# Loading a 3327 x 3327 int32 graph as bytes: casts on GpSimd replaced by casting transfers

## The chip, the cores and the metric

One core of one Trainium2 chip runs the kernel. The metric is device time in microseconds (us) of one execution; the kernel before was run three times.

## What is computed

Two layers on x (3327 rows of 256 floats), each a graph attention and a feed-forward part with residuals. The part that concerns us is the first graph attention, with two heads of 128 columns:

```python
e = leaky_relu(s1[:, None, :] + s2[None, :, :], 0.2)
e = where(adj[:, :, None] == 1, e, NEG)
att = softmax(e, axis=1)
h_prime = einsum('ijh,jhc->ihc', att, W3h)
```

`adj` is a 3327 x 3327 int32 matrix of zeros and ones (44.3 MB). After it come a mixture of 16 experts (two for each row), a second graph attention on the same graph with one head of 256 columns, and 30 steps of a recurrent feed-forward block.

## The kernel before

Rows are handled in 26 tiles of 128 (NT = 26, NP = 3328), and in pairs: tile 2c has the even rows and tile 2c+1 the odd rows of a stretch of 256. The last tile has 127 rows.

**Graph.** The whole graph stays in SBUF, transposed, as one byte for each edge (`adjT`, the tile `adj_pairs`), and both attentions read it there. `transpose_graph` (L227 to L251) fills it, one row tile i after the other, in two halves of 1664 and 1663 columns:

- L239: SP issues a load of int32 values into `raw` (three buffers, 832 KB each),
- L247, L249: GpSimd fills the padding of `bytes` (the last tile's last rows; the last column) with zeros,
- L250: GpSimd casts `raw` to 8-bit floats in `bytes` (two buffers),
- L251: when both halves are there, SP issues a DMA transpose of `bytes`, read as pairs of bytes, into the columns of `adj_pairs` that belong to row tile i.

**Projection.** Before the loop over edges, `project` normalizes x (L115, L116 on VectorE, the inverse deviation `rstd` at L106 on GpSimd, the scaling `xn` at L119 on VectorE), transposes it on TensorE (L149) and multiplies it by the weights (L157). VectorE puts the result into `wh` (L306) and the scores (L310, L311). `wv` and `shift` (L291 to L303) are made from weights that GpSimd's queue loads.

**Attention.** `attend` (L180 to L220) runs over row groups, in the first layer of 4, 6, 6, 6 and 4 tiles (L41), in each over heads and in each over the 26 tiles j of neighbours. One step j is: ScalarE makes `e` (L201, relu of a broadcast row of scores), VectorE adds and multiplies by the graph's bytes (L206, `pT`), TensorE multiplies each row tile of `pT` by `wh` (L211, `acc`). L206 reads for each j all columns of the group, so a group can't start before all its row tiles have been transposed: group 0 needs tiles 0 to 3, group 1 tiles 4 to 9, group 2 tiles 10 to 15, group 3 tiles 16 to 21, group 4 tiles 22 to 25. At the end of a group and head come the reciprocal (L219) and the residual (L320).

**Order.** Each engine executes its instructions in one order, which a scheduler lays down beforehand from the order of the program and planned durations; the code doesn't write it out. Casts of the graph and `rstd` of L106, for instance, stand mixed in GpSimd's order. An instruction that waits holds up all behind it on its engine. So also on the queues: SP's holds the loads of x (L70), of the graph, the transposes, and later the copies of x for the experts (L390); GpSimd's holds the loads of weights (L274, L286, L98).

Of the kernel before, what the change touches and what calls it, by code (L numbers as in the profile page):

```python
# [9 lines left out]
I32 = mybir.dt.int32  # L10
# [7 lines left out]
P = 128  # L18
# [8 lines left out]
def gat_moe_gat_recurrent_ffn(ctx: ExitStack, tc: tile.TileContext, a: dict, out: bass.AP):  # L27
    nc = tc.nc
    N, D = a["x"].shape
    KD = D // P  # L30
    NT = (N + P - 1) // P
    NP = NT * P
# [12 lines left out]
    def rows(t):  # L45
        return P if t < NT - 2 else (REST + 1 - t % 2) // 2

    def spread(n):

        cut = n - n % 16  # L50
        return [r for r in ((0, cut), (cut, n)) if r[0] < r[1]]

    def every_partition(ap, n):

        return bass.AP(tensor=ap.tensor, offset=ap.offset, ap=[[0, P], [1, n]])
# [83 lines left out]
    def project(wv, n_out, finish, ps_n, ps_p, work):  # L139

        for ts in groups:
            n = len(ts)
            xn = work.tile([P, G, D], F32, name="xn")
            normalized([x[:, t, :] for t in ts], [xn[:, j, :] for j in range(n)], EPS)
            hT = work.tile([P, KD, G * P], F32, name="hTg")
            for k in range(KD):
                pt = ps_n.tile([P, G * P], F32, name="pt")
                for j in range(n):
                    nc.tensor.transpose(pt[:, j * P : (j + 1) * P], xn[:, j, k * P : (k + 1) * P], ident)  # L149
                if k == 0:  # L150
                    nc.vector.tensor_copy(hT[:, k, : n * P], pt[:, : n * P])
                else:
                    nc.scalar.copy(hT[:, k, : n * P], pt[:, : n * P])
            for j, t in enumerate(ts):
                p = ps_p.tile([P, 512], F32, name="pp")
                for k in range(KD):
                    nc.tensor.matmul(  # L157
                        p[:, :n_out], lhsT=hT[:, k, j * P : (j + 1) * P], rhs=wv[:, k, :],
                        start=(k == 0), stop=(k == KD - 1),
                    )  # L160
                finish(t, p)
# [62 lines left out]
    adj_pairs = graph.tile([P, PAIRS, NP], BF16, name="adjT")  # L224
    adjT = adj_pairs.bitcast(FP8).rearrange("p c (i b) -> p c i b", b=2)

    def transpose_graph(ts, pools):  # L227

        raw_p, cast_p = pools
        half = NP // 2  # L230
        for i in ts:
            pr = rows(i)
            b = cast_p.tile([P, NP], FP8, name="bytes")
            for lo in (0, half):
                real = min(half, N - lo)
                raw = raw_p.tile([P, half], I32, name="raw")
                for r0, r1 in spread(pr):
                    first = i // 2 * 2 * P + i % 2 + 2 * r0
                    nc.sync.dma_start(  # L239
                        raw[r0:r1, :real],  # L240
                        bass.AP(
                            tensor=a["adj"].tensor, offset=a["adj"].offset + first * N + lo,
                            ap=[[2 * N, r1 - r0], [1, real]],
                        ),
                    )
                if pr < P:
                    nc.gpsimd.memset(b[96:P, lo : lo + half], 0.0)  # L247
                if real < half:
                    nc.gpsimd.memset(b[:, lo + real : lo + half], 0.0)  # L249
                nc.gpsimd.tensor_copy(b[:pr, lo : lo + real], raw[:pr, :real], saturate=False)  # L250
            nc.sync.dma_start(adj_pairs[:, :, i * P : (i + 1) * P], b.bitcast(BF16), transpose=True)  # L251


    with ExitStack() as st:
        H = 2
        C = D // H
        keep = st.enter_context(tc.tile_pool(name="keep0", bufs=1))
        wh = keep.tile([P, NT, H, C + 1], F32, name="wh")
        sc = Scores(keep, H)
        gpools = (  # L260
            st.enter_context(tc.tile_pool(name="raw", bufs=3)),
            st.enter_context(tc.tile_pool(name="cast", bufs=2)),
        )
        nc.vector.memset(wh[:, :, :, C : C + 1], 1.0)
        with ExitStack() as pre:
            work = pre.enter_context(tc.tile_pool(name="work0", bufs=2))
            hold = pre.enter_context(tc.tile_pool(name="hold0", bufs=1))
            ps_n = pre.enter_context(tc.tile_pool(name="ps0n", bufs=2, space=PSUM))
            ps_p = pre.enter_context(tc.tile_pool(name="ps0p", bufs=2, space=PSUM))
            ps_v = pre.enter_context(tc.tile_pool(name="ps0v", bufs=1, space=PSUM))  # L270

            def once(name, shape, src):
                t = hold.tile(shape, F32, name=name)
                nc.gpsimd.dma_start(t, src)  # L274
                return t

            w1 = once("gw1", [P, H, D], a["W1"].rearrange("(h c) d -> c h d", c=P))
            w2 = once("gw2", [P, H, D], a["W2"].rearrange("(h c) d -> c h d", c=P))
            aT = once("gaT", [P, 2, H], a["aT"].rearrange("(s c) h -> c s h", c=P))
            b1 = once("gb1", [P, H], a["b1"])  # L280
            b2 = once("gb2", [P, H], a["b2"])
            b3 = once("gb3", [P, D], every_partition(a["b3"], D))


            wv = hold.tile([P, KD, D + 2 * H], F32, name="wv")
            nc.gpsimd.dma_start(wv[:, :, :D], a["W3T"].rearrange("(k p) c -> p k c", p=P))  # L286
            for h in range(H):
                for k in range(KD):
                    for s, w in ((0, w1), (1, w2)):
                        pv = ps_v.tile([P, 1], F32, name="pv")  # L290
                        nc.tensor.matmul(  # L291
                            pv, lhsT=w[:, h, k * P : (k + 1) * P], rhs=aT[:, s, h : h + 1], start=True, stop=True
                        )
                        nc.vector.tensor_copy(wv[:, k, D + s * H + h : D + s * H + h + 1], pv)
            shift = hold.tile([P, H], F32, name="shift")
            for h in range(H):
                pv = ps_v.tile([P, 1], F32, name="pv")
                for s, b in ((0, b1), (1, b2)):
                    nc.tensor.matmul(
                        pv, lhsT=b[:, h : h + 1].to_broadcast([P, P]), rhs=aT[:, s, h : h + 1],  # L300
                        start=(s == 0), stop=(s == 1),
                    )
                nc.vector.tensor_copy(shift[:, h : h + 1], pv)  # L303

            def split0(t, p):
                nc.vector.tensor_tensor(  # L306
                    wh[:, t, :, :C], p[:, :D].rearrange("p (h c) -> p h c", h=H),
                    b3.rearrange("p (h c) -> p h c", h=H), ALU.add,
                )
                nc.vector.tensor_tensor(sc.s1[:, t, :], p[:, D : D + H], shift, ALU.add)  # L310
                nc.vector.tensor_copy(sc.s2[:, t, :], p[:, D + H : D + 2 * H])  # L311
                if t % G == G - 1 or t == NT - 1:
                    sc.finish(t - t % G, t + 1)

            project(wv, D + 2 * H, split0, ps_n, ps_p, work)
            transpose_graph(range(NT), gpools)

        def add_scaled(t, pr, h, po, r):
            xs = x[:pr, t, h * C : (h + 1) * C]
            nc.vector.scalar_tensor_tensor(xs, po, r, xs, op0=ALU.mult, op1=ALU.add)  # L320

        with ExitStack() as run:
            pools = (
                run.enter_context(tc.tile_pool(name="edge0", bufs=3)),
                run.enter_context(tc.tile_pool(name="ps0r", bufs=1, space=PSUM)),
                run.enter_context(tc.tile_pool(name="ps0o", bufs=2, space=PSUM)),
            )
            attend(sc, wh, H, groups0, 3, add_scaled, pools)
# [8 lines left out]
    with ExitStack() as st:  # L337
# [7 lines left out]
        first = hold.tile([P, SLOTS], F32, name="first")  # L345
# [3 lines left out]
        with ExitStack() as pre:  # L349
# [33 lines left out]
            for ts in groups:  # L383
# [30 lines left out]
                def gcol(name):  # L414
                    return gate.tile([P, G], F32, name=name)
# [12 lines left out]
                m1, r1, m2, r2 = gcol("m1"), gcol("r1"), gcol("m2"), gcol("r2")  # L428
# [183 lines left out]
    with ExitStack() as st:  # L612
# [31 lines left out]
        with ExitStack() as run:  # L644
            fin = run.enter_context(tc.tile_pool(name="fin2", bufs=2))

            def add_elu(t, pr, h, po, r):
# [9 lines left out]
            pools = (  # L657
                run.enter_context(tc.tile_pool(name="edge2", bufs=4)),
                run.enter_context(tc.tile_pool(name="ps2r", bufs=1, space=PSUM)),
                run.enter_context(tc.tile_pool(name="ps2o", bufs=1, space=PSUM)),  # L660
            )
# [145 lines left out]
```

## Time and profile before

| what | value |
|---|---|
| median of three runs | 2431.76 us (2431.38 to 2441.16) |
| profiled execution | 2433.84 us, its span 2432.1 us |
| TensorE busy | 2077.5 us, 85% |
| VectorE busy | 1544.4 us, 63% |
| ScalarE busy | 1068.8 us, 44% |
| GpSimd busy | 1024.5 us, 42% |
| mean granted TensorE clock | 0.942 of full speed |
| DMA traffic | 147.87 MB, HBM read 167.29 MB |

By stages: the projection ends at about 69 us, the first attention runs from there to about 426 us, the experts follow, then the second attention, and the recurrent block fills most of the last 900 us. The graph is loaded from 6.2 us (first load issued) to 227.5 us (last transpose issued). Sixteen DMA engines move the data; a load of half a row tile of the graph took a median of 6.8 us from issue to landing, a transpose 4.6 us.

How to read it: a group of instructions is given with its line, engine, operation, tiles (out<-in), shapes and count, then the busy time in us, the mean time of one in ns, and the time that its engine sat idle just before these instructions, with what ended it. The chain of work that ended last is followed back from the last instruction, at each step to what released it. "PEclk" is the share of full clock that TensorE was granted.

### The profile page before, as it was taken

The page shows a single profiled execution, that of the slowest core. Times are in us where ns is not written, and L with a number is a line of the kernel's source. Part 1 is how long each engine was busy: PE and PEld are TensorE (multiplying, and loading weights), DVE is VectorE, ACT ScalarE, POOL GpSimd, SP SyncE. Part 2 cuts the span into 40 slices and gives each one's busy share as a digit, 9 for nine tenths or more (in the row PEclk, how much of TensorE's full clock was granted, in tenths as well). Part 3 has the DMA queues.
Part 4 walks back from the last instruction along what each step waited for, and adds up shares of the span by engine and source line. Part 5 has one row for each costly group of instructions (what it writes and reads, how often), then busy time and mean ns, then how long its engine had stood idle before and what let it go on. Part 6 is the DMA issues. An engine that isn't in the chain of part 4 may idle for free.

```text
span 2432.1 us, 32383 instructions
## 1 busy us (share of the span) xinstructions
PE 2077.5 (85%) x10906; PEld 1695.3 (70%) x10906; DVE 1544.4 (63%) x4363; ACT 1068.8 (44%) x1373; POOL 1024.5 (42%) x743
## 2 busy tenths in 40 slices
PE   6889999610888888877999986999999999999998
PEld 4789999500444444545888875788888888888887
DVE  7899777610222222227555557988888888888888
ACT  1556566000222222212443344666666666666664
POOL 4544000233333333331000003777777777777774
PEclk9999999555999999998999997999999999999999
DMA  7987000101565665632000000000000000000001
GB/s 239 313 253 211 14 1 14 55 12 23 143 167 143 165 168 141 152 77 64 1 1 1 1 1 3 1 1 1 1 1 1 1 1 1 1 1 1 1 1 57
DMA packets 127889, 147.87 MB, mean 61 GB/s; under 512 B 61614, under 2 KB 97744, under 8 KB 127724
## 3 DMA queue, kind: packets, MB, share of 16 engines
q1 hardware_dynamic: 112364, 126.19, 17.0%
q0 software_dynamic: 15360, 19.62, 5.0%
q8 instruction: 87, 1.43, 0.2%
q14 instruction: 78, 0.64, 0.1%
HBM read 167.29 MB, written 19.30 MB: 77 GB/s over the span
## 4 chain that ended last, share of the span: by engine, by line
PE 62%; DVE 15%; DMA 10%; ACT 8%; issue 4%; POOL 1%; SPq 0%; ACTq 0%; DVEq 0%; POOLq 0%
PE acc L211 24%; PE po L745 19%; PE pa L589 5%; DMA lists<-number,ati 4%; DMA rows<-table_x,which 3%; ACT zT L741 3%; PE po L601 3%; DVE v L711 3%; DVE stats L737 3%; PE pt L739 3%; PE pb L589 3%; DVE pT L206 2%; DVE h L750 2%; ACT th L729 1%; PE pp L157 1%
## 5 line engine op out<-in xcount | busy, mean ns | idle before, releaser
L745 PE MATMUL po<-wc,zT 128*128 128x256 f32 x3120 | 711.0, 385 | 42.8 <-ACT zT L741 41.2
L745 PEld LDWEIGHTS po<-wc,zT 128*128 128x128 f32 x3120 | 586.8, 191 | 147.3 <-ACT zT L741 71.4
L211 PE MATMUL acc<-wh,pT 128*128 128x129 f32 (+1 forms) x4056 | 619.7, 315 | 53.1 <-DVE pT L206 49.4
L211 PEld LDWEIGHTS acc<-wh,pT 128*128 128x128 f32 x4056 | 570.7, 194 | 100.5 <-DVE pT L206 36.7
L206 DVE SCALAR_TENSOR_TENSOR pT<-e,part,adjT 128x512 f32<-128x512 f32 (+2 forms) x442 | 399.6, 921 | 165.4 <-PE acc L211 152.1
L731 POOL TENSOR_TENSOR th<-th,h 128x1024 f32<-128x1024 f32 (+1 forms) x210 | 463.7, 2209 | 82.7 <-ACT th L729 82.6
L201 ACT ACTIVATE e<-rb,minus,full 128x512 f32<-128x512 f32 (+2 forms) x442 | 358.5, 840 | 238.2 <-DVE pT L206 177.4
L750 DVE SCALAR_TENSOR_TENSOR h<-po,rr,bb 128x256 f32<-128x256 f32 x780 | 323.5, 477 | 32.5 <-PE po L745 26.5
L737 DVE BATCH_NORM_STATS2 stats<-z 128x6 f32<-128x256 f32 x780 | 286.4, 414 | 77.7 <-ACT z L732 77.7
L729 ACT ACTIVATE th<-h 128x1024 f32<-128x1024 f32 (+1 forms) x210 | 209.1, 996 | 283.8 <-DVE h L750 136.7
L720 POOL TENSOR_TENSOR rr<-v,neg_half 128x4 f32<-128x4 f32 (+1 forms) x210 | 204.5, 974 | 175.2 <-DVE v L716 173.6
L741 ACT COPY zT<-pt 128x1024 f32<-128x1024 f32 (+1 forms) x210 | 198.2, 945 | 76.7 <-PE pt L739 76.7
L732 ACT ACTIVATE z<-th 128x1024 f32<-128x1024 f32 (+1 forms) x210 | 210.4, 1002 | 9.1 <-DVE stats L737 6.7
L603 DVE TENSOR_SCALAR y<-po,col 128x256 f32<-128x256 f32 x67 | 32.4, 484 | 279.3 <-PE po L601 279.3
L739 PE MATMUL pt<-ident,z 128*128 128x128 f32 x1560 | 193.0, 275 | 16.4 <-ACT z L732 16.4
L739 PEld LDWEIGHTS pt<-ident,z 128*128 128x128 f32 x1560 | 180.1, 143 | 29.7 <-ACT z L732 17.8
L106 POOL TENSOR_TENSOR rstd<-ve,neg_half 128x4 f32<-128x4 f32 (+1 forms) x28 | 28.2, 1006 | 401.3 <-DVE ve L104 363.1
L604 POOL DMA_INDIRECT acc<-y,to x67 | 105.8, 1580 | 189.7 <-DVE y L603 97.1
L584 ACT COPY hT<-pt 128x256 f32<-128x256 f32 x67 | 24.9, 372 | 352.4 <-PE pt L583 219.9
L589 PE MATMUL pa<-ew,hT 128*128 128x512 f32 x268 | 146.9, 631 | 34.8 <-ACT hT L584 34.8
L711 DVE TENSOR_TENSOR v<-stats 128x4 f32<-128x4 f32 (+1 forms) x210 | 134.1, 638 | 7.1
L601 PEld LDWEIGHTS po<-ew,hidT 128*128 128x128 f32 x536 | 96.4, 189 | 57.6 <-ACT hidT L598 44.9
(180 smaller groups left out, 1618.9 us busy)
## 6 DMA issues: line engine op xcount, KB each, us to landing
ew<-in_w_dram SPq DMA_DIRECT2D x201, 512.0 KB
raw<-in_adj_dram SPq DMA_DIRECT2D x25, 832.0 KB, 6.8
raw<-in_adj_dram SPq DMA_DIRECT2D x25, 831.5 KB
acc<-x SPq DMA_DIRECT2D x26, 128.0 KB, 1.8
x<-acc SPq DMA_DIRECT2D x26, 128.0 KB, 3.3
table_x<-row SPq DMA_DIRECT2D x6, 520.0 KB, 3.1
x<-in_x_dram SPq DMA_DIRECT2D x6, 512.0 KB, 10.8
out_dram<-h SPq DMA_DIRECT2D x6, 512.0 KB, 2.8
```

What stands on the lines that cost most here:

```text
L201: nc.scalar.activation(e[:, : n * P], rb[:, :n, :].rearrange("p c q -> p (c q)"), AF.Relu, scale=sc.full[:, j, h : h + 1], bias=sc.minus[: ...
L206: nc.vector.scalar_tensor_tensor(pT[:, : n * P], e[:, : n * P], sc.part[:, j, h : h + 1], adjT[:, j // 2, ts[0] * P : (ts[-1] + 1) * P, j ...
L211: nc.tensor.matmul(po[c], lhsT=pT[:, c * P : (c + 1) * P], rhs=wh[:, j, h, :], start=(j == 0 and c % per_bank == 0), stop=(j == NT - 1), s ...
L589: nc.tensor.matmul(p, lhsT=hT[:, k, :], rhs=w[:, k, :], start=(k == 0), stop=(k == KD - 1))
L729: nc.scalar.activation(th[:, :n, :], hs, AF.Tanh, scale=1.0 / S)
L731: nc.gpsimd.tensor_tensor(th[:, :n, :], th[:, :n, :], hs, ALU.add)
L732: nc.scalar.activation(z[:, :n, :], th[:, :n, :], AF.Silu, scale=1.0 / S)
L737: nc.vector.bn_stats(stats[:, j, :], z[:, j, :])
L739: nc.tensor.transpose(pt[:, j, k, :], z[:, j, k * P : (k + 1) * P], ident)
L741: nc.scalar.copy(zT[:, :n, :, :], pt[:, :n, :, :])
L745: nc.tensor.matmul(po[:, j, :], lhsT=zT[:, j, k, :], rhs=wc[:, k, :], start=(k == 0), stop=(k == KD - 1),)
L750: nc.vector.scalar_tensor_tensor(h[:, ts[0] + j, :], po[:, j, :], rr[:, j : j + 1], bb, op0=ALU.mult, op1=ALU.add)
```

## The change

The loads of int32 into `raw` and GpSimd's casts are gone. GpSimd's queue issues transfers that read int32 from HBM and write 8-bit floats into `bytes`, so the transfer itself converts. Each row is cut at column 2048 into two transfers (2048 and 1279 columns), for all 128 rows of a tile at once; the last tile's 127 rows are split into 112 and 15, so it has four. The padding is filled first. `raw` and its three buffers vanish, `bytes` has four buffers instead of two. The transpose of L251 is as it was and stays on SP's queue.

```diff
-    def transpose_graph(ts, pools):
-
-        raw_p, cast_p = pools
-        half = NP // 2
+    def transpose_graph(ts, cast_p):
+
         for i in ts:
             pr = rows(i)
             b = cast_p.tile([P, NP], FP8, name="bytes")
-            for lo in (0, half):
-                real = min(half, N - lo)
-                raw = raw_p.tile([P, half], I32, name="raw")
-                for r0, r1 in spread(pr):
-                    first = i // 2 * 2 * P + i % 2 + 2 * r0
-                    nc.sync.dma_start(
-                        raw[r0:r1, :real],
+            if pr < P:
+                nc.gpsimd.memset(b[96:P, :], 0.0)
+            nc.gpsimd.memset(b[:, N:], 0.0)
+            for r0, r1 in spread(pr):
+                first = i // 2 * 2 * P + i % 2 + 2 * r0
+                for lo in range(0, N, 2048):
+                    hi = min(N, lo + 2048)
+                    nc.gpsimd.dma_start(
+                        b[r0:r1, lo:hi],
                         bass.AP(
                             tensor=a["adj"].tensor, offset=a["adj"].offset + first * N + lo,
-                            ap=[[2 * N, r1 - r0], [1, real]],
+                            ap=[[2 * N, r1 - r0], [1, hi - lo]],
                         ),
                     )
-                if pr < P:
-                    nc.gpsimd.memset(b[96:P, lo : lo + half], 0.0)
-                if real < half:
-                    nc.gpsimd.memset(b[:, lo + real : lo + half], 0.0)
-                nc.gpsimd.tensor_copy(b[:pr, lo : lo + real], raw[:pr, :real], saturate=False)
             nc.sync.dma_start(adj_pairs[:, :, i * P : (i + 1) * P], b.bitcast(BF16), transpose=True)
...
-        gpools = (
-            st.enter_context(tc.tile_pool(name="raw", bufs=3)),
-            st.enter_context(tc.tile_pool(name="cast", bufs=2)),
-        )
+        cast_p = st.enter_context(tc.tile_pool(name="cast", bufs=4))
...
-            transpose_graph(range(NT), gpools)
+            transpose_graph(range(NT), cast_p)
```

## The prediction

> **What bounds the kernel now.** I read the chain of work that ended last first, then the groups of instructions with shapes kept apart, for 70 to 232 us (the graph is being loaded) and for 232 to 440 us (the same loop, graph resident), then one tile's instructions, the chain in order of time, and the DMA packet records. The chain over the whole span says that TensorE sets the end, VectorE second:
>
> ```profile
> PE 62%; DVE 15%; DMA 10%; ACT 8%; issue 4%; POOL 1%; SPq 0%; ACTq 0%; DVEq 0%; POOLq 0%
> ```
>
> The change touches only what runs up to 232 us. In the groups of 70 to 232 us (count | busy us, mean ns | idle before) the edge products of L206 take 1352 and 1122 ns, beside GpSimd casts of 1.8 us:
>
> ```profile
> L206 DVE SCALAR_TENSOR_TENSOR pT<-e,part,adjT 128x768 f32<-128x768 f32 x64 | 83.1, 1352 | 3.5 <-PE acc L211 2.9 <-ACT e L201 0.6
> L206 DVE SCALAR_TENSOR_TENSOR pT<-e,part,adjT 128x512 f32<-128x512 f32 x52 | 56.0, 1122 | 2.4 <-ACT e L201 0.8
> L250 POOL CAST bytes<-raw 128x1664 fp8e4<-128x1664 int32 x19 | 35.3, 1860 | 30.4 <-DMA raw<-in_adj_dram 30.4
> ```
>
> The same instructions from 232 us on, with GpSimd idle:
>
> ```profile
> L206 DVE SCALAR_TENSOR_TENSOR pT<-e,part,adjT 128x768 f32<-128x768 f32 x93 | 94.0, 1017 | 27.8 <-PE acc L211 25.5 <-ACT e L201 2.2
> L206 DVE SCALAR_TENSOR_TENSOR pT<-e,part,adjT 128x512 f32<-128x512 f32 x52 | 38.6, 750 | 5.8 <-PE acc L211 0.5 <-ACT e L201 0.2
> ```
>
> Min/median/max of the 52 products in the first row group (69 to 132 us), then in the last (374 to 426 us), which has the same shape:
>
> ```profile
> L206 DVE SCALAR_TENSOR_TENSOR pT<-e,part,adjT x52: 737/751/2078, 70.0 to 130.2; 128x512 f32<-128x512 f32 x52
> ```
>
> ```profile
> L206 DVE SCALAR_TENSOR_TENSOR pT<-e,part,adjT x52: 732/752/753, 375.4 to 423.3; 128x512 f32<-128x512 f32 x52
> ```
>
> The medians agree; the first group has a tail up to 2078 ns, as long as a cast. A product that meets a cast waits it out. The tail is on the chain, and so are two stalls in the projection before it (start, us):
>
> ```profile
> 39.02 3.23 DVE xn L119 x2
> ...
> 54.24 1.46 DVE xn L119
> ...
> 75.65 2.02 DVE pT L206
> ...
> 80.88 2.06 DVE pT L206
> ```
>
> **The change, part by part.** Each sum is made against the profiled execution (2433.84 us, span 2432.1), 2.1 us over the median of 2431.76.
>
> *Casts removed (52 of L250, 91.5 us of GpSimd).* Row group 0 runs from 69.23 to 132.23 us on the chain, 63.0; group 4, same size without casts, from 374.57 to 425.65, 51.1: 11.9 us less. Late next there is PE: its 104 products of one head take 23.4 us, VectorE's 26 x 0.75 = 19.5, ScalarE's 26 x 0.78 = 20.2. Group 1 (six tiles) takes 132.23 to 214.95, 82.7; groups 2 and 3 take 79.0 and 79.7: 3.4 us less. VectorE loses 64 x 335 ns = 21 us to casts in the six-tile groups, but PE is the longer engine there (some 36 us a head against 26 x 1.02 = 26.5), so most of it is hidden. Together -15.3.
>
> In the projection the xn scalings of L119 have a median of 408 ns; on the chain the pair at 39.02 takes 3.23 instead of 0.73 us, the one at 54.24 1.46 instead of 0.40, the pair at 56.1 1.5 instead of 0.73: -4.4. PE ran dry at both places and then had a clock of 0.52 (43.4 to 46.8 us) and 0.50 (57.0 to 63.8); at that clock eight products of L157 took 3.41 us, elsewhere 1.92. That is 1.5 + 2 x 0.95 = 3.4 us that may go or stay; I take half, -1.7.
>
> *Transfers moved from SP to GpSimd's queue.* 54 issues leave SP; 54 come to GpSimd, two a tile (four for the last). GpSimd's plain issues in the trace take 0.54 to 0.89 us, so some 40 us, against 91.5 of casts. Behind them in GpSimd's order stand the rstd of L106; two are on the chain (37.96, 52.33), each perhaps behind one issue: +0.75 each, +1.5. A tile's issue now also waits for one of four "bytes" buffers, that is for a transpose four tiles back; behind that wait stand later issues and rstd. The memsets (26 of 0.10 us, 3 us for the last tile) stay. On SP only transposes and x loads stay; a transpose now waits for a transfer instead of a cast. The first transfers can start behind the weight loads, at 6.4 us, beside the x loads rather than behind them on SP; x may land later; VectorE idles 2.3 us for PE's shift at 26 to 28 us, which hides that much. I take nothing.
>
> Do issues stall VectorE as casts do? Lowest price nothing, highest the same share, 40/91.5 = 44% of the gain given back. The rows nearest: three issues from 16.82 to 18.68 us, beside which xn took 0.46 and 0.75 for two, the undisturbed times within 0.06. I take nothing. [...]
>
> *The cast inside the transfer: the unknown.* No row shows a casting DMA. Packet records: a plain 6656-byte packet took 252 ns (median) on SP's queue, 4096 bytes 159 ns on GpSimd's, so the same 26 bytes/ns from either; a 256-byte transpose packet 18 ns; a 1024-byte packet of the accumulating scatter of L604, the only DMA here that computes, 101 ns against 45 plain. Per tile and DMA engine there are 8 rows of 13.3 KB and 104 transpose packets (1.9 us). Low end, plain rate: 8 x 504 ns + 1.9 = 5.9 us a tile; in the trace two tiles take 14 us with the DMA engines full, 7. High end by the nearest row, the accumulating one: 13308/1024 x 101 = 1313 ns a row, 10.5 + 1.9 = 12.4 us a tile. At X us a tile, tile k (from 0) has landed at 6.4 + (k+1)X + 4.6 (transposes land in 4.6). With the gains above, group 0 starts at 64.6 and group 1 at 115.7; it needs tile 9, so 11 + 10X <= 115.7: X up to 10.5 costs nothing, because the matmuls of earlier groups hide the loading (groups 2 to 4 allow 11.5 or more). I take the plain end, X about 7: the casting transfer reads each byte once and writes a quarter of it, while the accumulating one reads two streams (2 x 45 = 90 of its 101 ns), so it too looks bound by reading.
>
> **Sum:** -11.9 - 3.4 - 4.4 - 1.7 + 1.5 = -19.9 us; 2433.8 becomes 2413.9, and on the median 2431.8 becomes 2412.
>
> **Rivals.**
> 1. *The cast runs like the accumulating scatter* (X about 12.4): group 1 waits for tile 9 until 135 us, ends at 135 + 79.3 = 214.3 against 214.95 now, and nothing is gained: 2431. For it: the only computing row. Against: two streams in it.
> 2. *Issues block VectorE like casts:* 56% of 19.9, 11 us: 2421. Against: the rows at 17 us.
> 3. *GpSimd's order:* an rstd of the next stage's layernorm (at 141.5 us now; GpSimd sat 11.7 us before it with casts behind it) waits for the end of group 0. If fewer than ten tiles are issued before it, tiles 8 and 9 come 9 (until rstd) + 14 + 4.6 = 28 us after group 0's end at 115.7, and group 1 starts at 143.5 instead of 132.2: 11.3 - 3.4, so 2440. Against: now thirteen tiles pass before it.
> 4. *The casting transfer is slower than any row* and the loop starves; this one is slower than before. It decides from X = 12.9 (group 3 needs tile 21: 11 + 22X = 294, its start now); group 4 (373.6 now) is held beyond 14. At X = 16 group 3 starts at 363 and ends at 442, group 4 starts 69 us late: 2501; at 23 (half the accumulating rate) tile 25 lands at 609, 235 us late: 2667. For it: a packet of 8 KB that is converted element by element appears in no row. Against: the accumulating row, already read-bound, would have to be undercut.
> That the change leaves the stalls alone is out: the GpSimd instructions that cause them are gone.
>
> **How the numbers follow.** About 0.5% (12 us) is what a measurement of this kernel can tell from no change. Forecast 0.60 (2406 to 2420: all clock and early stalls gone, or only 12 us); rival 1 0.09, rival 2 0.07, rival 3 0.05, rival 4 0.19. Faster by over 0.5% (under 2419.6): 0.60. Within: 0.09 + 0.07 + 0.05 = 0.21. Slower: 0.19. The range goes from 2406 to 2450, which takes in rivals 1 to 3 and the mild part of rival 4 (X up to 13.8, about 0.03), and leaves out some 0.16.
>
> **What would show it.** Right: products of L206 at 750 and 1017 ns from the start; group 0 in about 51 us, group 1 in 79; xn at 0.41; GpSimd issues under 1 us; transposes 7 us apart. Wrong: L206 idle for a DMA of adjT (rivals 1, 4; packets of 8192 bytes over 700 ns), L206 over 1 us beside issues (2), GpSimd idle on rstd with issues behind it before tile 9 (3).

## The result: slower, and what the profile after shows

The changed kernel takes 2467.53 us (median of four runs, 2465.26 to 2472.09); the kernel before took 2436.2 beside it (2431.38 to 2441.16). The ratio is 1.0131, 95% interval 1.0099 to 1.0162: slower by some 31 us, where 20 us faster was forecast. The profiled execution took 2466.5 us, its span 2464.7.

The chain that ended last, over the whole span: DMA gained, VectorE lost.

```profile
PE 63%; DVE 13%; DMA 12%; ACT 7%; issue 3%; POOL 1%; SPq 0%; ACTq 0%; POOLq 0%; DVEq 0%
```

What was forecast for the edge products is there. Groups of the whole first attention (118 to 460 us), then xn in the projection (min/median/max):

```profile
L206 DVE SCALAR_TENSOR_TENSOR pT<-e,part,adjT 128x768 f32<-128x768 f32 x156 | 157.4, 1018 | 44.8 <-PE acc L211 43.2 <-ACT e L201 1.6
L206 DVE SCALAR_TENSOR_TENSOR pT<-e,part,adjT 128x512 f32<-128x512 f32 x104 | 77.3, 751 | 12.9 <-ACT e L201 1.0 <-PE acc L211 0.5
```

```profile
L119 DVE TENSOR_SCALAR xn<-x,mv,rstd x26: 403/407/531, 17.2 to 106.5; 128x256 f32<-128x256 f32 x26
```

All products have the undisturbed times; group 0 takes 117.40 to 168.38 us, 51.0, group 1 from there to 246.74, 78.4. But look at the last start of xn: 106.5 us, where it was 58.9. The projection ends 48 us later. The chain in order of time (start, us) says what it waited for:

```profile
16.92 0.53 POOL bytes L239
17.45 6.24 DMA bytes<-in_adj_dram
23.74 77.85 DMA adjT<-bytes x8
...
102.18 1.07 POOL bytes L239 x2
103.25 1.06 POOL rstd L106
104.34 0.41 DVE xn L119
```

78 us of the chain are transposes of the graph, each of which sets free a buffer for GpSimd's next issue, and at the end stands not an edge product but an rstd of the projection. GpSimd in order of time shows how (idle before, and what ended it, in brackets):

```profile
44.56 0.10 POOL L234 MEMSET bytes<- 128x1 fp8e4 x1 [2.97 <-DMA adjT<-bytes]
44.80 1.07 POOL L239 DMA_DIRECT2D bytes<-in_adj_dram  x2
58.07 0.10 POOL L234 MEMSET bytes<- 128x1 fp8e4 x1 [12.20 <-DMA adjT<-bytes]
58.31 1.07 POOL L239 DMA_DIRECT2D bytes<-in_adj_dram  x2
59.60 0.10 POOL L234 MEMSET bytes<- 128x1 fp8e4 x1 [0.22 <-DMA adjT<-bytes]
60.05 1.06 POOL L239 DMA_DIRECT2D bytes<-in_adj_dram  x2 [0.35 <-issue]
61.11 1.05 POOL L106 TENSOR_TENSOR rstd<-ve,neg_half 128x4 f32<-128x4 f32 x1
```

GpSimd sleeps 12 us for a buffer, with the fifth rstd close behind in its order. That rstd ran at 37.96 us before, now at 61.11; the sixth and seventh ran from 52.33, now from 103.25. In the kernel before, GpSimd waited just ahead of them for VectorE, not for a buffer:

```profile
37.96 1.03 POOL L106 TENSOR_TENSOR rstd<-ve,neg_half 128x4 f32<-128x4 f32 x1 [9.80 <-DVE ve L104]
52.32 1.67 POOL L106 TENSOR_TENSOR rstd<-ve,neg_half 128x4 f32<-128x4 f32 x2 [8.63 <-DVE mv L116]
```

The waits of the first 120 us put a number on it (total us, times, longest):

```profile
DVE xn L119 <- POOL rstd L106: 53.3, 2, 29.7
PE pt L149 <- DVE xn L119: 52.2, 2, 29.9
```

The first of these two in the kernel before, up to 70 us:

```profile
DVE xn L119 <- POOL rstd L106: 1.3, 2, 0.8
```

The order is laid down beforehand: with four buffers the scheduler put the issues of nine tiles ahead of the fifth rstd and those of sixteen ahead of the sixth and seventh. Tile 8, the ninth, needs the buffer of tile 4, tile 15 that of tile 11.

### The profile page after: what moved, and what is told of

Read it like the earlier page. It is cut to its first block, busy times and chain, and to the rows that moved or that the text cites. A ratio compares the mean times of both kernels' runs of the same rounds, so it can differ in the third digit from the quotient of the medians.

```text
span 2464.7 us, 32356 instructions
## 1 busy us (share of the span) xinstructions
PE 2071.9 (84%) x10906; PEld 1697.1 (69%) x10906; DVE 1502.4 (61%) x4363; ACT 1071.6 (43%) x1373; POOL 963.1 (39%) x744
## 2 busy tenths in 40 slices
DMA packets 127893, 114.67 MB, mean 47 GB/s; under 512 B 61618, under 2 KB 101075, under 8 KB 127728
## 3 DMA queue, kind: packets, MB, share of 16 engines
HBM read 167.29 MB, written 19.30 MB: 76 GB/s over the span
## 4 chain that ended last, share of the span: by engine, by line
PE 63%; DVE 13%; DMA 12%; ACT 7%; issue 3%; POOL 1%; SPq 0%; ACTq 0%; POOLq 0%; DVEq 0%
PE acc L211 24%; PE po L737 19%; PE pa L581 5%; PE po L593 4%; DMA lists<-number,ati 4%; ACT zT L733 3%; PE pb L581 3%; DMA adjT<-bytes 3%; DMA rows<-table_x,which 3%; DVE v L703 3%; DVE stats L729 3%; PE pt L731 3%; DVE h L742 2%; ACT th L721 1%; ACT z L724 1%
## 5 line engine op out<-in xcount | busy, mean ns | idle before, releaser
L211 PE MATMUL acc<-wh,pT 128*128 128x129 f32 (+1 forms) x4056 | 613.0, 315 | 41.7 <-DVE pT L206 38.2
L206 DVE SCALAR_TENSOR_TENSOR pT<-e,part,adjT 128x512 f32<-128x512 f32 (+2 forms) x442 | 363.8, 829 | 181.8 <-PE acc L211 165.5
```

Source lines behind the costliest of these rows:

```text
L206: nc.vector.scalar_tensor_tensor(pT[:, : n * P], e[:, : n * P], sc.part[:, j, h : h + 1], adjT[:, j // 2, ts[0] * P : (ts[-1] + 1) * P, j ...
L211: nc.tensor.matmul(po[c], lhsT=pT[:, c * P : (c + 1) * P], rhs=wh[:, j, h, :], start=(j == 0 and c % per_bank == 0), stop=(j == NT - 1), s ...
```

## Experiments

**Theory 1 (queue):** rstd 5 to 7 stand in GpSimd's order behind issues that wait for a "bytes" buffer. **Theory 2 (traffic):** the casting transfers, or the work of issuing them, hold up the projection as such. **Theory 3 (buffers):** four buffers are too few to load fast. Ratios are to the kernel before, run beside each.

**e2: the waiting issues behind the last rstd.** rstd stays on GpSimd, the buffers stay four; only the order changes (queue order, no added wait). `last_rstd` collects the rstd instructions.

```diff
...
-            transpose_graph(range(NT), cast_p)
+            transpose_graph(range(4), cast_p)
+            with tc.issue_after(last_rstd[-1]):
+                transpose_graph(range(4, NT), cast_p)
```

> The changed kernel, with the transfers of tiles 4 to 25 put into GpSimd's order behind the last of the projection's seven inverse deviations (rstd, L106); tiles 0 to 3, which find free buffers, stay ahead of them. Theory 1 (the queue: rstd 5 to 7 stood behind issues that wait for a bytes buffer, and held the projection by some 50 us): the last rstd runs at about 52 us instead of 104, group 0 starts at 64 to 69 us instead of 118, products of L206 stay at 750 and 1018 ns, and the time is about 2412, ratio to before 0.99. Theory 2 (the casting transfers themselves hold the projection, through DMA or descriptor traffic): the four first tiles still load during the projection, so it ends much later than 69 us and the time stays above 2440. Theory 3 (four buffers are too few for the loading): no gain, since the buffers are the same: about 2467.

Measured: 2419.1 us against 2443.86, ratio 0.9899 (0.9879 to 0.9919). GpSimd now waits for VectorE, not for transposes, ahead of its rstd, and the waiting issues follow:

```profile
36.80 1.03 POOL L108 TENSOR_TENSOR rstd<-ve,neg_half 128x4 f32<-128x4 f32 x1 [8.94 <-DVE ve L106]
47.39 1.67 POOL L108 TENSOR_TENSOR rstd<-ve,neg_half 128x4 f32<-128x4 f32 x2 [9.56 <-DVE mv L118]
49.02 0.10 POOL L236 MEMSET bytes<- 128x1 fp8e4 x1
49.05 1.24 POOL L241 DMA_DIRECT2D bytes<-in_adj_dram  x2
```

Group 0 starts at 61.47 us (117.40 in the changed kernel, 69.23 before; 64 to 69 expected). Theory 3 falls, since the buffers are the same four. Theory 2 is weakened only, since fewer tiles load during the projection than in the changed kernel; e7 decides it.

**e7: the same cure by another way.** Statistics and rstd of all seven groups are computed ahead of the projection's loop:

```diff
+            for ts in groups:
...
+                nc.gpsimd.tensor_tensor(r[:, :n], ve[:, :n], neg_half[:, :n], ALU.pow)
+                known.append((mv, r))
-            project(wv, D + 2 * H, split0, ps_n, ps_p, work)
+            project(wv, D + 2 * H, split0, ps_n, ps_p, work, known)
```

> The changed kernel, with the statistics and the rstd of all seven row groups computed ahead of the projection's loop, so that GpSimd has all of them behind it after two and a half tiles of transfers; the transfers keep their early start. Theory 1: the same cure by another way; group 0 starts at 64 to 72 us (VectorE does 26 statistics first, about 5 us more before its first scaling), and the time is 2408 to 2418. Theory 2: projection ends late, above 2440. Theory 3: about 2467.

Measured: ratio 0.9897 (0.9876 to 0.9917); the last rstd is done by 23.3 us, group 0 starts at 59.00. That is earlier than the 64 to 72 expected. It makes e2's gain without holding any transfer back, and with it theory 2 falls: up to 62 us e7 has issued 18 casting transfers, as many as the changed kernel, and they take as long from issue to landing (median 9.3 us against 9.8). Yet e7's chain lies on TensorE for at least 25.5 us between 30 and 58 us, while in the changed kernel TensorE is busy for 10.4 us between 30 and 59.

**e8, control: the kernel before with e7's edit.**

> The kernel before with the rstd of all seven groups ahead of the projection, as e7 has them, and nothing else changed. Theory 1: its two rstd on the chain waited for VectorE, not for a queue (the scalings waited 1.3 us for them), so this alone gives at most 3 us: ratio 0.998 to 1.001. If early rstd alone is the gain of e7: 0.990.

Measured: ratio 0.998 (0.9967 to 0.9994). Early rstd alone is worth 0.2%; with the casts on GpSimd the products of four tiles still average 1081 ns. The other 0.8% of e7 comes with the casting transfers, since e7 and e8 differ by the change alone.

**e3: two, three and twelve buffers.** The scheduler packs more issues ahead of the rstd where it has more buffers, so theory 1 forecasts from the order where the seventh rstd must wait. The edit changes `bufs=4` of the pool "cast".

> The changed kernel with two bytes buffers instead of four. The planned order then has the fifth rstd behind five and a half tiles of issues, the sixth behind eight, the seventh behind ten (with four buffers: nine, sixteen, sixteen). Theory 1: the seventh rstd waits for the transpose of tile 7, at about 80 to 95 us although loading is slower; group 0 starts at 95 to 107 us instead of 118: 2443 to 2456, faster than the changed kernel. Theory 3 (too few buffers): slower than 2467.

> The changed kernel with three bytes buffers. The planned order has the fifth rstd behind seven and a half tiles, the sixth behind twelve, the seventh behind fourteen and a half. Theory 1: the seventh waits for the transpose of tile 11 (with two buffers tile 7, done before 73.6 us; with four tile 11, 101.7 us): about 92 to 100 us, group 0 starts at 102 to 112, 2450 to 2462, ratio to before 1.006 to 1.011: two buffers beat three, three at best equal four. If more buffers simply loaded faster: better than two buffers (0.999).

> The changed kernel with twelve bytes buffers. The planned order has the fifth rstd behind eleven and a half tiles, which now need no wait, the sixth behind eighteen and the seventh behind twenty-two. Theory 1: the seventh waits for the transpose of tile 9, at the loading rate of the changed kernel about 96 us; group 0 starts at about 105 to 110: 2453 to 2460, hardly better for three times the buffers. Theory 3: the waits are gone and the forecast gain comes back, about 2412.

| buffers | tiles issued ahead of rstd 5, 6, 7 | rstd 7 starts, us | group 0 starts, us | ratio (interval) |
|---|---|---|---|---|
| 2 | 5.5, 8, 10 | 73.56 | 83.15 | 0.999 (0.9977 to 1.0002) |
| 3 | 7.5, 12, 14.5 | 98.28 | 107.03 | 1.0089 (1.0062 to 1.0116) |
| 4 (the change) | 9, 16, 16 | about 104.3 | 117.40 | 1.0131 (1.0099 to 1.0162) |
| 12 | 11.5, 18, 22 | 121.30 | 131.21 | 1.0341 (1.0318 to 1.0365) |

Two buffers beat three. Between three and four the intervals of the times overlap, but group 0 starts 10 us earlier with three. So more buffers are worse, as the order says and against theory 3. Three came as forecast in ratio, rstd 7 and group 0. I had two buffers too slow (forecast 2443 to 2456; 0.999 of 2436.2 is 2434), because loading with two is hardly slower (last transpose issued at 196.9 us, with four at 186.5). The forecast for twelve failed (2453 to 2460; 1.0341 of 2436.2 is 2519). Part is the rstd: the first twelve tiles find a free buffer, but from the ninth transfer on each issue of these tiles waits for an earlier transfer to land (18 waits, 27.1 us), which put rstd 5 at 52.5 us. After that GpSimd waited another 49 us for transposes, and rstd 7 came at 121 us instead of 96. The greater part is another wait, of the same kind on another engine:

```profile
ACT e L201 <- DVE pT L206: 44.7, 3, 43.2
...
DVE empty L357 <- DMA adjT<-bytes: 43.1, 1, 43.1
```

The memset of `empty`, a tile of the next stage, stands in VectorE's order inside group 0 and waits until the last transpose, at 182 us, is done with a "bytes" buffer; I read this as memory used again, since twelve buffers may take the place where that tile lies, but no run tries it apart.

**e5 and e6: what held VectorE up.** On e2, 52 GpSimd instructions are put back, two a tile: in e5 casts of a still 128x1664 int32 tile (they read SBUF and write), in e6 memsets of the same size (they only write). Nothing reads what they write. The lines of both kernels stand together here; each kernel has one of the last two.

```diff
...
+            for lo in (0, 1):
+                junk = junk_p.tile([P, NP // 2], FP8, name="junk")
+                nc.gpsimd.tensor_copy(junk, still, saturate=False)   # e5
+                nc.gpsimd.memset(junk, 0.0)                          # e6
```

> The kernel of e2 (issues behind the last rstd) with 52 GpSimd casts of 128x1664 int32 put back, two a tile, reading a still buffer and writing a junk tile that nobody uses, so that no transfer waits for them. Theory 1 (VectorE's products were held up by a GpSimd instruction that reads SBUF): L206 has its tail to 2 us again while the graph loads, group 0 loses up to 11.9 us and group 1 up to 3.4, and most of e2's gain goes: ratio to before 0.994 to 0.998. Rival (the gain came from the transfers and the longer buffers, not from the missing casts): ratio stays at 0.990.

> The same with 52 GpSimd memsets of the same junk tile (128x1664 bytes, about as long as a cast, SBUF written and not read). If only a reading GpSimd instruction holds up the products: L206 stays at 750 and 1018 ns, ratio 0.990 as in e2. If any busy GpSimd does: as e5.

Measured: e5 1.0102 (1.008 to 1.0125), e6 0.9971 (0.9956 to 0.9986), against 0.9899 of e2. The groups from 55 to 240 us, e5 and then e6:

```profile
L208 DVE SCALAR_TENSOR_TENSOR pT<-e,part,adjT 128x768 f32<-128x768 f32 x53 | 78.6, 1519 | 8.9 <-PE acc L213 8.3 <-ACT e L203 0.6
L251 POOL CAST junk<-still 128x1664 fp8e4<-128x1664 int32 x44 | 73.1, 1662 | 0.1
L208 DVE SCALAR_TENSOR_TENSOR pT<-e,part,adjT 128x512 f32<-128x512 f32 x52 | 55.2, 1091 | 6.3 <-PE acc L213 2.5 <-ACT e L203 0.2
```

```profile
L208 DVE SCALAR_TENSOR_TENSOR pT<-e,part,adjT 128x768 f32<-128x768 f32 x78 | 78.7, 1017 | 21.3 <-PE acc L213 20.9 <-ACT e L203 0.4
L251 POOL MEMSET junk<- 128x1664 fp8e4 x44 | 67.6, 1536 | 0.1
L208 DVE SCALAR_TENSOR_TENSOR pT<-e,part,adjT 128x512 f32<-128x512 f32 x52 | 38.7, 752 | 6.5 <-ACT e L203 0.2
```

GpSimd is nearly as long busy in both (73.1 and 67.6 us in these instructions), yet only beside the casts are the products longer: 1091 instead of 752 ns and 1519 instead of 1017. The casts read SBUF, the memsets don't; that the reading is what holds the products up I infer from these two runs, and no other GpSimd instruction was tried. I expected e5 to lose less (0.994 to 0.998). Its span is 44.8 us longer than that of e2, and 13.1 of these lie ahead of group 0, which starts at 74.61 us. The rest I put down to the casts waiting for no load and running in bunches, one every 2.1 us; that was not tried apart. And I expected e6 to lose nothing, but it starts group 0 at 73.37 us, 11.9 later than e2; from there on it is no slower (2350.7 us to the end of the span, e2 2353.3). Its chain shows the place:

```profile
18.58 3.87 DVE xn L121 x2
...
22.52 3.88 DVE xn L121 x2
...
62.46 2.76 DVE xn L121 x2
```

The scalings of xn are longer beside the memsets too: two take 3.9 us instead of 0.73, and the longest single one takes 2.43 us, in e2 0.53.

## Why the prediction was wrong, point by point

- *Casts removed, -11.9 and -3.4:* right. Group 0 takes 51.0 us (forecast 51.1), group 1 78.4 (79.3); the products are long again where e5 puts casts back (1091 and 1519 ns).
- *xn, -4.4, and half the clock loss, -1.7:* xn is at its 407 ns. Where the queue is cured, the projection ends before 61.5 us (e2) instead of 69.2: 7.7 less, where these two terms make 6.1 (in e2 no graph issue stands just ahead of these rstd, so the +1.5 doesn't enter). The size was a little low. Of the two slow stretches of TensorE one is left in e2: from 52.3 us on 16 products of the projection take 5.21 us, where 8 take 1.75 elsewhere; so half was a fair guess.
- *Casting transfer at the plain rate:* right, and the great uncertainty was none. The packet of 2048 elements (8192 bytes read) took a median of 322 ns, that of 1279 elements 209 ns: 25 bytes/ns, where the plain packets before had 26. Tiles come 6.4 us apart, in bunches of three about 19 us apart. Rivals 1 and 4 are out. Rival 2 also: issues took 517 to 613 ns, xn beside them at most 531, and the products average 751 and 1018.
- *Transfers moved from SP to GpSimd's queue, +1.5:* this is the step that failed. The prediction said that behind a wait for a buffer "stand later issues and rstd", and then charged each rstd with an issue's own duration, 0.75 us, and not with the wait. They cost 53.3 us of waiting, and group 0 began 48.2 us late. The sum of what was measured: +48.2 - 12.0 (group 0) - 4.3 (group 1) = +31.9, and the span is longer by 32.6.
- *Rival 3 (GpSimd's order)* came nearest, but took the wrong rstd: it looked at the next stage's at 141.5 us, and in the wrong direction, issues behind an rstd instead of an rstd behind issues; so it was priced at +8 us and given 0.05. Two things kept the wait away before. Most waits of the loading stood on SP (its transposes waited 68.0 us for casts, up to 14.0 at a time), and a blocked SP blocks no rstd. GpSimd waited for loads and buffers too, but only 9.4 us in the first 70, with three and a half tiles ahead of the last rstd. That this order would stay was tacitly assumed, without a reason; the changed one has sixteen tiles there.
- *Slower, 0.19:* this chance stood on rival 4 alone, a slow casting transfer, and that did not come. What did come had no price, so it is luck that the direction was covered at all.

The cured versions e2 and e7 show what the change is worth without that wait: 2436.2 x 0.99 = 2411.8, beside the forecast 2412. They beat both kernels. That the two figures meet is in part luck: the gain is 24.4 us from 2436.2, the forecast was 19.9 from 2431.8.

## What to carry to other kernels

When a transfer moves to a computing engine's queue, its waits move there too. Here a wait of 12.2 us for a buffer stood ahead of an rstd of 1.05 us on GpSimd, and VectorE waited 53.3 us, in two waits, for such rstd. So list the small instructions behind such waits, and ask which the critical path needs. Give the waiting issues their place by hand, behind the last instruction that the path needs (e2), or compute what is needed before they begin (e7). More buffers are no cure where a scheduler turns them into more issues ahead of the same instruction.

## What the runs showed of the hardware

- The casting transfers read at about the rate of the plain ones: 322 ns for 8192 bytes of int32 (25 bytes/ns), where the plain 6656 bytes took 252 (26). The profile counts what they write: 256 KB for a tile's first transfer, and 114.67 MB of DMA traffic in all where it was 147.87, while the HBM reads stay at 167.29 MB.
- With GpSimd memsets of 1.54 us beside them (e6), VectorE's products of four tiles take 752 ns, as without; with casts of 1.66 us beside them (e5) 1091. One scaling of xn takes up to 2.43 us in e6 and 2.51 in e5, at most 0.53 in e2. Why memsets lengthen the scaling and not the product, no run shows.
